# Gate and up of the shared MLP's first chunk as seven block products, in the last two token blocks

## Chip, cores and metric

The kernel runs on one core of a Trainium2 chip, in float32. The metric is the device time of one execution in microseconds (us). TensorE (PE) multiplies into PSUM, VectorE (DVE) and ScalarE (ACT) read PSUM and write SBUF, GpSimd (POOL) issues the indirect DMAs, and SyncE (SP) issues the others.

## What is computed

Two layers are applied to 2048 tokens of 512 features. The change touches the last part alone: the mixture-of-experts layer that ends the second one. Cut to what matters:

```
gu_s = x2 @ shared_w_gate_up.T            # shared MLP: 512 inner features
g_s, u_s = split(gu_s, 2)
shared_out = silu(g_s) * u_s @ shared_w_down.T
...                                       # router: top 2 of 16 experts
out_e = (silu(g) * u) @ w_down[e]         # 16 experts of 128 inner features
moe_out = einsum('eth,te->th', out_e, combine)
x = x + moe_out + shared_out
```

## The kernel before

**Tiles.** The tokens lie in four blocks of 512 columns (`tb` 0 to 3), the 512 features in four chunks of 128 partitions, all in one SBUF tile, `xall`. The shared MLP's 512 inner features are four chunks `j` of 128; `sw[j]` holds the weights of a chunk: columns 0 to 511 are gate, 512 to 1023 up, and the rest down.

**A chunk, plain.** `gate_up` (matmuls at L785) makes gate and up of chunk 0: two times four calls of 128x128 weights against 512 tokens, each result in one PSUM bank. A float32 call is two matmul instructions, so these are 16.

**A chunk from seven products.** Chunks 1 to 3 go through `seven`. Gate and up are taken as two rows of blocks, the features as two halves, the tokens as two halves of 256; the two-by-two block product is then seven block products and some additions (the scheme of Strassen in Winograd's form). It takes 14 calls against 256 tokens, 28 instructions (L1064). It needs sums of weight blocks, S2, S3 and S4, which `combine_shared(j)` makes with four DVE subtractions and additions, and differences of token blocks, `diffs[tb]`. The sum S1 is written over the first half of up in `sw[j]`, so that after `combine_shared(j)` a plain product of this chunk is no longer possible. The seven products come in four PSUM banks: the first is copied to SBUF by ACT (L1068), the others are added in by seven DVE instructions (L1070 to L1079).

**After either form,** ACT takes silu of gate (L1123), DVE multiplies by up (L1124), and `down` multiplies the result by the down weights, into four PSUM banks that gather all four chunks of a block (L1099; eight instructions a chunk). `down` of a chunk is issued after the products of the next, so that PE has work while ACT and DVE finish. At the end of a block DVE adds the four banks to the residual `x1` (L1144).

**Banks.** PSUM gives these stages three pools: `ps_mm` and `ps_td` of two banks each, taken in turn, and `ps_acc` of four for `down`. A plain chunk takes both banks of `ps_mm`; a chunk of seven products takes two of `ps_mm` and two of `ps_td`. A bank can be written again when its last reader is through.

**The end of the kernel, where the change lies.** Blocks 0 and 1 are computed earlier, beside the router. Then come the tiles of the experts (`worked`), which store their rows in `yd` in DRAM, and after them block 2, block 3 and the sum of the experts' rows. `shared(2, behind=sums)` and `shared(3, ...)` run the loop over `j` and call `sums(j)` after each chunk's product. For three rows of tokens or so at a time, `sums` weighs what was gathered (`weighed`: L1428, and L1429, which frees a buffer) and starts the next gathers (`rows_of`: a DVE memset of one column, L1419, then an indirect DMA on POOL, L1421; 32 gathers of 128 rows in all). The first six gathers are started ahead of block 2. The gathered tiles `g1` have six buffers, so a later gather waits for a weighing. `routed` runs midway through block 3: it transposes the weighed rows on PE (L1448, 64 instructions in 16 tiles, through `ps_mm` and `ps_td`) and DVE adds them to `x1` (L1449).

**Order.** Up to the experts, the order of PE, DVE and ACT is the program's own. From the experts on, a scheduler orders each engine's instructions; each engine then works its list from front to back. The weight sums of chunk 3, which were made early and put away in DRAM, are loaded again by SP (L1408) into a pool at the right end of SBUF, which lies where the experts' weights were.

Of the kernel before, what the change touches and what calls it, by code (L numbers as in the profile page):

```python
# [9 lines left out]
F32 = mybir.dt.float32  # L10
# [7 lines left out]
P = 128  # L18
# [11 lines left out]
NS1 = 4  # L30
# [13 lines left out]
BW = L // 2  # L44
# [59 lines left out]
def kernel(ctx: ExitStack, tc: tile.TileContext, a: dict, out: bass.AP):  # L104
    nc = tc.nc
    mm, tt, ts = nc.tensor.matmul, nc.vector.tensor_tensor, nc.vector.tensor_scalar
# [25 lines left out]
    s4 = wl0.tile([P, 5, H], F32, name="s4")  # L132
# [105 lines left out]
    def run(*streams):  # L238

        while streams:  # L240
            streams = [x for x in streams if next(x, run) is not run]
# [34 lines left out]
    start = small(1)  # L276
# [13 lines left out]
    pos = cst[:, C_POS : C_POS + NQ]  # L290
# [498 lines left out]
    def differ(g):  # L789
# [8 lines left out]
        tt(t3, b22, b12, ALU.subtract)  # L798
        tt(t4, b21, t2, ALU.subtract)

    def combine_shared(j):


        if j == NS1 - 1:
            assert len(ssw) == j - 1
            ssw.append(dif.tile([P, 4 * BW], F32, tag="t", name="ssw_made"))
        a11, a12, a21, a22 = (sw[j][:, i * BW : (i + 1) * BW] for i in range(4))
        s2, s3, s4 = (ssw[j - 1][:, i * BW : (i + 1) * BW] for i in range(3))
        yield tt(s3, a11, a21, ALU.subtract)
        yield tt(a21, a21, a22, ALU.add)  # L810
        yield tt(s2, a21, a11, ALU.subtract)
        yield tt(s4, a12, s2, ALU.subtract)
        if j == NS1 - 1:
            nc.sync.dma_start(shared_d, ssw[j - 1][:, 0 : 3 * BW])
# [59 lines left out]
    class Group:  # L874
# [6 lines left out]
        def down(self, j, at):  # L881
            for half in range(2):
                lo = half * TW
                for s in range(2):
                    mm(  # L885
                        self.zp[half][s][:, 0 : DW - TW],
                        at[:, 1 - half, :],
                        wn[:, j, s, lo : lo + DW - TW],
                        start=(j == 0),
                        stop=(j == NF - 1),  # L890
                    )
# [161 lines left out]
    def seven(tb, j, banks, si, at, done):  # L1053

        b11, b12, b21, b22 = quarters(tb)
        t1, t2, t3, t4 = diffs[tb]
        gate, up = (x.rearrange("p (k t) -> p k t", k=2) for x in (si, at))

        def products(k, *parts):
            ps = bank(banks[k % len(banks)], f"sgu_{tb}_{j}_{k}").rearrange("p (k t) -> p k t", k=2)  # L1060
            for i, (w, x) in enumerate(parts):
                w = sw[j][:, w * BW :] if w < 4 else ssw[j - 1][:, (w - 4) * BW :]
                for c in range(2):
                    mm(ps[:, i, :], w[:, c * P : (c + 1) * P], x[:, c, :], start=(c == 0), stop=(c == 1))  # L1064
            return ps

        ps = products(0, (0, b11), (6, b22))
        nc.scalar.copy(gate, ps)  # L1068
        ps = products(1, (1, b21), (4, t2))
        tt(up[:, 0], gate[:, 0], ps[:, 1], ALU.add)  # L1070
        tt(gate[:, 0], gate[:, 0], ps[:, 0], ALU.add)  # L1071
        tt(gate[:, 1], gate[:, 1], up[:, 0], ALU.add)
        done("gate", j)
        ps = products(2, (3, t4), (5, t3))
        tt(up[:, 1], up[:, 0], ps[:, 1], ALU.add)
        tt(up[:, 0], up[:, 1], ps[:, 0], ALU.add)  # L1076
        ps = products(3, (2, t1))
        tt(gate[:, 1], gate[:, 1], ps[:, 0], ALU.add)
        tt(up[:, 1], up[:, 1], ps[:, 0], ALU.add)  # L1079
# [3 lines left out]
    def shared(tb, behind=None, midway=None, hooks=None, first=None):  # L1083

        op = []
        hooks = hooks or {}

        def done(*step):  # L1090
            if step in hooks:
                hooks[step]()

        def down(j, at):
            if j == 0:
                op.extend(bank(ps_acc, f"op_{tb}_{o}") for o in range(NC))
            for o in range(NC):
                i = 2 * L + o * P
                mm(op[o], sw[j][:, i : i + P], at, start=(j == 0), stop=(j == NS1 - 1))  # L1099
            done("down", j)  # L1100

        before = None
        for j in range(NS1):
            if j > 0:
                si = glu.tile([P, TB], F32, tag="si", name=f"ssi_{tb}_{j}")
                at = glu.tile([P, TB], F32, tag="at", name=f"sat_{tb}_{j}")
                seven(tb, j, (ps_mm,) if hooks else (ps_mm, ps_mm, ps_td, ps_td), si, at, done)
                pair = [si, at]
            elif first is not None:
                pair = first()  # L1110
            else:
                banks = ps_mm if hooks else (ps_mm, ps_td)[j % 2]
                pair = []
                for which in range(2):
                    pair.append(bank(banks, f"sgu_{tb}_{j}_{which}"))
                    gate_up(pair[-1], tb, j, which)
                    if which == 0:
                        done("gate", j)
            done("products", j)
            if j == 0:  # L1120
                si = glu.tile([P, TB], F32, tag="si", name=f"ssi_{tb}_{j}")
                at = glu.tile([P, TB], F32, tag="at", name=f"sat_{tb}_{j}")
            nc.scalar.activation(si, pair[0], AF.Silu)  # L1123
            product = tt(at, si, pair[1], ALU.mult)  # L1124
            if j == 0 and tb == 1:
                diffs[tb] = in_place_of(0)
                run(differing(tb, diffs[tb]))
            if j == 0:
                x1 = pools[(1, 0, 2, 2)[tb]].tile([P, NC, TB], F32, tag="acc", name=f"x1_{tb}")
                nc.sync.dma_start(x1, x1d[tb])  # L1130
                acc.append(x1)
            done("up", j)
            if behind is not None:
                with tc.issue_after(product.ins):
                    behind(j)
            if before is not None:
                down(j - 1, before)
            before = at
            if j == 1 and midway is not None:
                midway()  # L1140
        down(NS1 - 1, before)

        for o in range(NC):
            tt(x1[:, o, :], x1[:, o, :], op[o], ALU.add)  # L1144
# [261 lines left out]
    late = ctx.enter_context(tc.tile_pool(name="late", bufs=1, side="right"))  # L1406
    ssw[-1] = late.tile([P, 3 * BW], F32, name="ssw_late")
    nc.sync.dma_start(ssw[-1], shared_d)  # L1408
    with tc.tile_pool(name="fin", bufs=NT) as fin:
        order = [q * NTB + tb for tb in range(NTB) for q in range(NTB)]  # L1410
        pairs = []

        def rows_of(lo, hi, held=True):

            for n in order[lo:hi]:
                g = [fin.tile([P, L], F32, tag=f"g{k}", name=f"g{k}_{n}", bufs=(NT, 6)[k]) for k in range(2)]
                for k in range(2):
                    if held:
                        nc.vector.memset(g[k][:, 0:1], 0.0)  # L1419
                    at = bass.IndirectOffsetOnAxis(ap=posi[:, k, n : n + 1], axis=0)  # L1420
                    nc.gpsimd.indirect_dma_start(g[k], None, yd[:, :], at)  # L1421
                pairs.append(g)

        def weighed(lo, hi):

            for i in range(lo, hi):
                n, g = order[i], pairs[i]
                ts(g[0], g[0], shr[:, 0, n : n + 1], None, ALU.mult)  # L1428
                stt(g[0], g[1], shr[:, 1, n : n + 1], g[0], ALU.mult, ALU.add)  # L1429

        cuts = (0, 0, 3, 6, 9, 13, NT)

        def sums(j):
            weighed(cuts[j], cuts[j + 1])
            rows_of(3 * (j + 1), min(3 * (j + 2), NT))

        rows_of(0, 3, held=False)
        shared(2, behind=sums)

        def routed():  # L1440

            for tb in range(NTB):
                for o in range(NC):
                    ps = bank((ps_mm, ps_td)[o % 2], f"moe_{tb}_{o}")
                    by_head = ps.rearrange("p (h b) -> p h b", b=B)
                    for q in range(4):
                        src = pairs[tb * 4 + q][0][:, o * P : (o + 1) * P]
                        nc.tensor.transpose(by_head[:, :, q * 2 * GB : (q + 1) * 2 * GB], src, ident)  # L1448
                    tt(acc[tb][:, o, :], acc[tb][:, o, :], ps, ALU.add)  # L1449
                    if tb < NTB - 1:  # L1450
                        nc.sync.dma_start(out[tb, :, o, :], acc[tb][:, o, :])

        shared(3, behind=lambda j: sums(4 + j) if j < 2 else None, midway=routed)
        for o in range(NC):
            nc.sync.dma_start(out[3, :, o, :], acc[3][:, o, :])
# [95 lines left out]
```

## Time and profile before

| | |
|---|---|
| median of 4 runs | 1032.94 us (1031.3 to 1036.56) |
| profiled execution, own time | 1031.51 us |
| its span | 1029.7 us |
| PE busy | 991.5 us, 96% |
| DVE busy | 648.2 us, 63% |
| ACT busy | 213.3 us, 21% |
| POOL busy | 169.8 us, 16% |
| mean granted PE clock | 0.998 |

The profile is of one execution. Its own time is 1.8 us more than its span, which goes from the first instruction to the last. Times in a row are in us from the span's start, unless marked ns. In a row of the timeline, the first number is the start and the second the time to the end of the last of its instructions; a bracket at the end tells how long the engine had been idle and what ended that. "remote" and "another core or an unknown queue" stand for a wait whose end the profile can't put down to an instruction that it has. Matmuls are pipelined, so their rows overlap: the step from one to the next is what one costs.

### The profile page before, as it was taken

The numbers are of one execution on the slowest core, as the hardware profiler recorded it, in microseconds if no ns is written. First come the engines' busy times: TensorE is split into PE (matmuls) and PEld (weight loads), VectorE is DVE, ScalarE is ACT, GpSimd is POOL, SyncE is SP. The second block draws the span as 40 slices with busy tenths as digits, with TensorE's granted clock in tenths as the row PEclk, the third lists the DMA queues.
The fourth block names the chain that finished last, engine by engine and source line by source line (L and its number), as shares of the span: only waits on it lengthen the run. The fifth ranks groups of instructions, "written<-read, shape, count | busy, mean of one in ns | idle before, by whom it ended". The sixth has DMA issues, their size and how long they took to land. (4 is left out here: it accounts for less than half of the span.)

```text
span 1029.7 us, 16926 instructions
## 1 busy us (share of the span) xinstructions
PE 991.5 (96%) x6256; PEld 792.8 (77%) x6256; DVE 648.2 (63%) x1974; ACT 213.3 (21%) x439; POOL 169.8 (16%) x189
## 2 busy tenths in 40 slices
PE   3999999999999999999999999999999999999898
PEld 1777656888898889988899888897757777776566
DVE  6655567886666776666766757775864443334485
ACT  2322111121221311223112122212101222221000
POOL 2131001210301202102012021000001222223530
PEclk9999999999999999999999999999999999999999
DMA  6666408685656756746467466532920455546452
GB/s 183 194 218 230 134 21 303 232 295 176 224 183 195 243 165 210 252 154 232 150 219 256 161 200 229 180 108 71 417 120 23 133 167 170 172 156 217 140 175 98
DMA packets 64210, 190.62 MB, mean 185 GB/s; under 512 B 8512, under 2 KB 11616, under 8 KB 63488
## 3 DMA queue, kind: packets, MB, share of 16 engines
q1 hardware_dynamic: 49360, 138.30, 39.1%
q0 software_dynamic: 14176, 51.16, 15.9%
q8 instruction: 52, 0.85, 0.3%
q14 instruction: 30, 0.25, 0.1%
q10 hardware_dynamic: 592, 0.07, 0.1%
HBM read 158.35 MB, written 31.15 MB: 184 GB/s over the span
## 5 line engine op out<-in xcount | busy, mean ns | idle before, releaser
L885 PE MATMUL zp<-wn,at 128*128 128x288 f32 x704 | 185.4, 406 | 0.4 <-DVE at L984 0.4
L819 PE MATMUL gu<-t,w 128*128 128x128 f32 x1056 | 150.6, 279 | 1.0 <-DVE gus L966 0.9
L885 PEld LDWEIGHTS zp<-wn,at 128*128 128x128 f32 x704 | 127.1, 190 | 28.6 <-DVE at L984 0.6
L819 PEld LDWEIGHTS gu<-t,w 128*128 128x128 f32 x1056 | 134.8, 191 | 16.4 <-DVE gus L966 8.6
L444 POOL DMA_INDIRECT wa<-in_la,row_a x64 | 61.4, 959 | 305.3 <-issue 185.1
L982 ACT ACTIVATE si<-gus 128x256 f32<-128x256 f32 x88 | 36.8, 418 | 346.6 <-DVE gus L980 346.6
L819 PE MATMUL gum<-xall,w 128*128 128x128 f32 x704 | 93.3, 275 | 0.0
L819 PEld LDWEIGHTS gum<-xall,w 128*128 128x128 f32 x704 | 85.6, 192 | 0.0
L960 DVE TENSOR_TENSOR los<-los 128x512 f32<-128x512 f32 (+1 forms) x72 | 46.6, 647 | 55.9 <-ACT los L839 54.1
L1327 PE MATMUL egu<-wall,zx 128*128 x336 | 80.6, 383 | 0.4 <-issue 0.4
L1327 PEld LDWEIGHTS egu<-wall,zx 128*128 128x128 f32 x336 | 60.5, 189 | 20.0 <-ACT zx L1318 10.4
L966 DVE TENSOR_TENSOR gus<-gu,los 128x512 f32<-128x512 f32 x88 | 60.6, 689 | 23.8 <-PE gu L819 11.0
L984 DVE TENSOR_TENSOR at<-si,gus 128x256 f32<-128x256 f32 x88 | 37.5, 426 | 48.4 <-ACT si L982 47.3
L1308 POOL DMA_INDIRECT zr<-zd,tok x42 | 39.8, 948 | 159.4 <-PE zrp L1316 86.3
L839 ACT COPY los<-lo 128x512 f32<-128x512 f32 (+1 forms) x96 | 47.5, 558 | 65.3 <-PE lo L836 62.2
L1099 PE MATMUL op<-sat,sw 128*128 128x512 f32 x128 | 58.3, 596 | 2.7 <-DVE sat L1124 2.4
L589 PE MATMUL main<-yT,w 128*128 128x512 f32 x128 | 58.4, 599 | 0.0
L836 PEld LDWEIGHTS lo<-rs,wb 64*128 64x128 f32 x704 | 42.6, 187 | 17.0 <-issue 11.2
L836 PE MATMUL lo<-rs,wb 64*128 64x128 f32 x704 | 48.0, 279 | 6.9 <-DVE gus L980 6.2
L819 PE MATMUL gu<-xall,w 128*128 128x128 f32 x352 | 53.7, 275 | 0.0
L819 PE MATMUL gum<-t,w 128*128 128x128 f32 x352 | 53.7, 275 | 0.0
L1347 DVE COPY eys<-ey 128x512 f32<-128x512 f32 x42 | 29.1, 692 | 29.7 <-PE ey L1345 29.7
(316 smaller groups left out, 1456.3 us busy)
## 6 DMA issues: line engine op xcount, KB each, us to landing
w<-sums_d SPq DMA_DIRECT2D x77, 512.0 KB
w<-in_cw SPq DMA_DIRECT2D x77, 384.0 KB
wall<-in_xw SPq DMA_DIRECT2D x16, 768.0 KB
yd<-eys SPq DMA_DIRECT2D x42, 256.0 KB
g<-kpad SPq DMA_DIRECT2D x15, 512.0 KB
w<-in_cw SPq DMA_DIRECT2D x11, 512.0 KB
sums_d<-w SPq DMA_DIRECT2D x9, 512.0 KB
xall<-in_xT SPq DMA_DIRECT2D x4, 1024.0 KB
```

The costliest lines, as they stand in the source:

```text
L444: nc.gpsimd.indirect_dma_start(to, None, src, at)
L589: mm(ps, w0[:, c, o * P : (o + 1) * P], yT[:, c, :], start=(c == 0), stop=(c == NC - 1),)
L819: mm(to, block(n, i)[:, c * P : (c + 1) * P], x[:, c], start=(c == 0), stop=(c == 1))
L836: mm(banks[which][:, at : at + P], wb[mine, lo : lo + P], r[mine, half, :], start=True, stop=True)
L839: nc.scalar.copy(to[:, first - j : first - j + n, 2 * which : 2 * which + 2], src)
L885: mm(self.zp[half][s][:, 0 : DW - TW], at[:, 1 - half, :], wn[:, j, s, lo : lo + DW - TW], start=(j == 0), stop=(j == NF - 1),)
L960: tt(lo[:, :, i], lo[:, :, i], lo[:, :, less], ALU.subtract)
L966: tt(flat, ps, adapters[:, j % 4].rearrange("p k t -> p (k t)"), ALU.add)
L984: tt(at, si, flat[:, TG:], ALU.mult)
L1099: mm(op[o], sw[j][:, i : i + P], at, start=(j == 0), stop=(j == NS1 - 1))
L1308: nc.gpsimd.indirect_dma_start(zr, None, zd[:, :], bass.IndirectOffsetOnAxis(ap=tok[:, t : t + 1], axis=0))
L1327: mm(ps[:, 0:256], x[:, c, :], wflat()[:, bass.ds(start + c * 256, 256)], start=(c == 0), stop=(c == NC - 1))
```

## The change

Block 2 now takes its chunks in the order 1, 2, 0, 3. After the product of its first chunk (chunk 1), DVE makes the weight sums of chunk 0, from the weights in SBUF, into a new tile, `ssw_first`. Chunk 0 of block 2 (now third) and of block 3 (still first) then go through `seven` as the other chunks do. Blocks 0 and 1 keep the plain form. `sums`, the load of `x1` and `routed` go by a chunk's position in the order, no longer by its number.

```diff
+    first_sums = []
+
+    def sums_of(j):
+        return ssw[j - 1] if j > 0 else first_sums[0]
+
     def combine_shared(j):
...
-        s2, s3, s4 = (ssw[j - 1][:, i * BW : (i + 1) * BW] for i in range(3))
+        s2, s3, s4 = (sums_of(j)[:, i * BW : (i + 1) * BW] for i in range(3))
         yield tt(s3, a11, a21, ALU.subtract)
         yield tt(a21, a21, a22, ALU.add)
         yield tt(s2, a21, a11, ALU.subtract)
...
-                w = sw[j][:, w * BW :] if w < 4 else ssw[j - 1][:, (w - 4) * BW :]
+                w = sw[j][:, w * BW :] if w < 4 else sums_of(j)[:, (w - 4) * BW :]
...
+        order = (1, 2, 0, 3) if tb == 2 else range(NS1)
+
         def down(j, at):
-            if j == 0:
+            if not op:
                 op.extend(bank(ps_acc, f"op_{tb}_{o}") for o in range(NC))
             for o in range(NC):
                 i = 2 * L + o * P
-                mm(op[o], sw[j][:, i : i + P], at, start=(j == 0), stop=(j == NS1 - 1))
+                mm(op[o], sw[j][:, i : i + P], at, start=(j == order[0]), stop=(j == order[-1]))
             done("down", j)
...
-        for j in range(NS1):
-            if j > 0:
+        for pos, j in enumerate(order):
+            plain = j == 0 and tb < 2
+            if not plain:
...
                 seven(tb, j, (ps_mm,) if hooks else (ps_mm, ps_mm, ps_td, ps_td), si, at, done)
...
-            if j == 0:
+            if plain:
                 si = glu.tile([P, TB], F32, tag="si", name=f"ssi_{tb}_{j}")
...
-            if j == 0:
+            if pos == 0:
                 x1 = pools[(1, 0, 2, 2)[tb]].tile([P, NC, TB], F32, tag="acc", name=f"x1_{tb}")
                 nc.sync.dma_start(x1, x1d[tb])
...
                 with tc.issue_after(product.ins):
-                    behind(j)
+                    behind(pos)
             if before is not None:
-                down(j - 1, before)
+                down(order[pos - 1], before)
             before = at
-            if j == 1 and midway is not None:
+            if pos == 1 and midway is not None:
                 midway()
-        down(NS1 - 1, before)
+        down(order[-1], before)
...
     nc.sync.dma_start(ssw[-1], shared_d)
+    first_sums.append(late.tile([P, 3 * BW], F32, name="ssw_first"))
...
-        shared(2, behind=sums)
+        def first_then_sums(j):
+            if j == 0:
+                run(combine_shared(0))
+            sums(j)
+
+        shared(2, behind=first_then_sums)
```

## The prediction

> **What bounds the kernel now.** The page comes first: PE is busy 96% of the span, so the time is the length of PE's work plus the places where PE stands still. The change lies behind the experts, so the second view is the busy time by stretch: block 2 (932.70 to 979.54 us), block 3 up to the end of `routed` (to 1006.37), and the rest, with a piece of the second stretch by itself. The columns are the stretch, its length, then busy time and count of PE, PEld, DVE, ACT and POOL, the granted clock, the DMA share and GB/s.
>
> ```profile
> 932.70:979.54 46.84, 41.78 (x137) 26.50 (x135) 22.70 (x71) 4.14 (x7) 23.94 (x24) 0.96 0.59 190
> 979.54:1006.37 26.83, 26.83 (x125) 18.01 (x123) 21.84 (x43) 1.81 (x3) 7.59 (x8) 1.00 0.59 192
> 1006.37:1029.70 23.33, 19.23 (x75) 13.60 (x73) 11.01 (x23) 2.44 (x4) 0.00 (x0) 0.99 0.19 69
> ...
> 997.40:1006.40 9.00, 9.00 (x60) 6.69 (x59) 9.00 (x16) 0.00 (x0) 0.00 (x0) 1.00 0.78 290
> ```
>
> Two things are to be seen. In block 2 PE is idle for 5.06 of 46.84 us and its clock is below 1. In the last 9 us of `routed` DVE is as full as PE.
>
> The chain of waits tells why block 2 ends when it does (start, length, what).
>
> ```profile
> 951.98 11.23 another core or an unknown queue
> 963.30 0.42 DVE sat L1070
> ...
> 964.52 1.56 another core or an unknown queue
> 966.10 0.43 DVE sat L1075
> ...
> 975.25 0.70 DVE sat L1124
> 976.00 3.70 PE op L1099 x8
> 979.70 6.87 PE sgu L785 x16
> 986.57 6.04 PE sgu L1064 x28
> ```
>
> DVE stands still for 11.23 us ahead of the first addition of the block's third chunk, and 1.56 us later. The products it needs were issued on PE at 951.63 and 953.36, so PE was long through. I call this the **hold**: what PE finished at about 953 and 955 us is seen by DVE at 963.2 and 966.1. Its cause isn't in the profile. What stands beside it is a stream of 18 gathers on POOL, back to back from 940.62 to 963.36; their queue is 64% busy from 962 to 964 us and 18% from 964 to 970. A second stream, 12 gathers from 971.57 to 987.00, has no hold.
>
> PE's timeline shows what the hold costs.
>
> ```profile
> 960.25 1.03 PE L1064 MATMUL sgu<-xall,ssw_late 128*128 128x256 f32 x4
> 964.23 2.07 PE L1064 MATMUL sgu<-xall,sw 128*128 128x256 f32 x4 [2.96 <-issue]
> 966.10 1.78 PE L1064 MATMUL sgu<-xall,ssw_late 128*128 128x256 f32 x4
> 967.71 1.03 PE L1064 MATMUL sgu<-xall,sw 128*128 128x256 f32 x4
> ...
> 976.00 3.70 PE L1099 MATMUL op<-sat,sw 128*128 128x512 f32 x8 [2.10 <-DVE sat L1124]
> ```
>
> PE waits 2.96 us for a bank that DVE hasn't read; the next eight matmuls take 967.71 - 964.23 = 3.48 us instead of 8 x 0.216 = 1.73; and PE waits 2.10 us for the last `down`. Together 2.96 + 1.75 + 2.10 = 6.81 us.
>
> **The change, part by part.** *Products.* Each of the two blocks loses 16 instructions of L785 (6.87 us in the chain, 0.429 each) and gains 28 of L1064 (6.04 us, 0.216 each). That is 0.83 us less PE work in each block, 1.66 in both. PSUM banks: two products move to `ps_td`, whose last readers ahead of both places are done.
>
> *DVE and ACT.* Each block gains seven DVE additions of 128x256 (0.42 us in their row, 2.9 in all) and one copy on ACT (0.59). What matters is when the chunk's product is ready, since `weighed` is queued behind it on DVE. For a chunk alone, the timeline of DVE and PE has it:
>
> ```profile
> 986.67 0.69 DVE L1124 TENSOR_TENSOR sat<-ssi,sgu 128x512 f32<-128x512 f32 x1 [4.82 <-issue]
> ...
> 1006.48 1.03 PE L1064 MATMUL sgu<-xall,sw 128*128 128x256 f32 x4
> ...
> 1013.90 0.69 DVE L1124 TENSOR_TENSOR sat<-ssi,sat 128x512 f32<-128x512 f32 x1 [0.43 <-ACT ssi L1123]
> ```
>
> From PE's start of a chunk of seven to its product are 1013.90 - 1006.48 = 7.42 us. In block 3, where PE starts at 979.54, the product then starts at 986.96, not 986.67: 0.29 us late. The other additions fall into the 4.82 us in which DVE is idle today.
>
> *Sums of chunk 0.* Four DVE instructions of 128x256, 4 x 0.42 = 1.7 us once, in the list between the products of chunks 1 and 2. PE starts chunk 1 in effect at 933.6 (932.70, and 0.86 for the last experts' matmul that stands among its first ones), so its product ends at about 933.6 + 7.42 + 0.69 = 941.7, and the sums by 943.5. Chunk 2's additions can start when its second product is through, at 933.6 + 6.04 + 3.46 + 0.1 = 943.2, and are 0.3 us late, which the products behind cover. PE needs the sums at 933.6 + 2 x 6.04 + 3.43 (a `down`) + 0.86 = 950.0, within the first product of chunk 0: 6.5 us of cover, so nothing. Six memsets for gathers 7 to 12 stand between them, at 942 to 943.5 instead of 941.34; POOL comes to the first of these gathers at 948.14, so 4.6 us of cover. The third row of `weighed` still waits for its gather, as now (950.58). SP's and POOL's lists keep their order, and no DMA is added.
>
> [...] The gathers beside SBUF-only work of DVE take longer in the trace:
>
> ```profile
> 946.89 0.95 POOL L1421 DMA_INDIRECT g<-yd,posi  x1 [0.30 <-issue]
> 948.14 1.32 POOL L1421 DMA_INDIRECT g<-yd,posi  x1 [0.30 <-issue]
> 949.76 1.06 POOL L1421 DMA_INDIRECT g<-yd,posi  x1 [0.30 <-issue]
> ```
>
> Beside five such instructions of `weighed` two gathers together lose 0.48 us. [...] By the row it is 4/5 of 0.48, 0.4 us, for the first stream; nothing on the path waits for these gathers, so I add nothing.
>
> *Block 2 in sum.* PE comes 0.83 us sooner to the point where it waits for a bank. DVE frees the bank only after the hold. Bounds: 0, if the hold ends at a fixed time with the gathers, and 0.83, if it moves with PE; below nothing, 1.7 by the second rival. I take 0, since the gathers don't move. Behind the hold the same list follows (additions, three weighings, additions, product), so the last `down` starts at 976.0 as now.
>
> *Block 3 in sum.* From 986.67 to 1007.7 DVE has hardly a gap, so it ends `routed` 0.29 us later. PE would come to the products of chunk 2 at 1006.48 - 0.83 = 1005.65, but needs a bank of `ps_mm`, freed by the 13th of the 16 additions of L1449. The first starts at 997.41, the other 15 run from 998.67 in steps of 0.60, so this one ends at 998.67 + 11 x 0.60 + 0.69 = 1005.96 today, at 1006.25 after. PE starts at about 1006.3: 0.18 us sooner, and 0.65 of the 0.83 is lost to DVE.
>
> **Sum:** 0 + 0.18 = 0.2 us less: 1031.3 for an execution like the profiled one. That one is 1.4 us under the median of the four runs, so I forecast **1032.7 us** as the median.
>
> **Rivals.** *The hold is gone.* It shows once in two streams of gathers, and the change gives the third chunk other instructions at other times. Against it: all runs before lie between 1031.3 and 1036.56, none near 1024, so it seems to come each time; and the first stream stays as it is. It would give back 6.81, and 0.83 + 0.18 of the change's own: 7.8 us less, 1025.1. It is faster by 0.76%.
>
> *A second spell of half clock.* The matmuls after PE's idle time of 2.96 us took 0.427 us instead of 0.216; after 2.10 us ahead of the last `down` they didn't. If PE works off its 0.83 us ahead of that wait while DVE doesn't move, the idle time is 2.93, next to the bad one. The spell lasted 3.4 us and costs half of it, 1.7: 1.5 us slower in all, 1034.4. It decides between 2.10 and 2.96 us. [...]
>
> *A hold in the second stream.* These 12 gathers run beside chunk 0 of block 3, which now has three more results for DVE to wait for. The first hold ended 2.7 us behind the last issue of its stream (963.36 to 966.1). One from 983.2, where the first addition is due, to 987.0 + 2.7 = 989.7 costs up to 6.5 us, and the weighings and `routed` stand behind it on DVE: 1032.7 + 6.5 = 1039.2. It decides as soon as DVE's first addition starts later than 984. Today ACT's silu starts there in time, which speaks against it.
>
> *The change doesn't do what it says.* The lists of instructions exclude this: PE, DVE and ACT differ only from block 2 on, DVE by 7 + 7 + 4 instructions.
>
> **Numbers.** Hold as now, 0.55: 1032.7, and 1031 to 1035 with the scatter of the runs. Hold gone or most of it, 0.26: 1025.1. Half clock, 0.10: 1034.4. Hold in the second stream, 0.09: 1039.2. Leaving out the last and the tails, the range is 1024.2 to 1036.5. Half a per cent, 5.2 us, is about what a measurement of this kernel can tell from no change. Faster by more: the second case nearly whole, 0.25. Slower by more: the last and some scatter, 0.09. Within: 0.66.
>
> **What would show it.** Right: L785 is gone behind 932 us, a chunk 0 takes 6.04 us on PE, DVE's unknown wait stands ahead of chunk 0 in block 2 and ends near 963, PE's idle time there grows to about 3.8 us, and DVE's additions in `routed` end near 1008. Wrong: block 2 ends at other than 979.5, by the hold (earlier) or by matmuls at 0.43 us per 256 tokens behind the last wait (later).

## The result and the profile after

The changed kernel took **1035.71 us** (median of 44 runs, 1029.30 to 1042.82); the kernel before, beside it, 1033.63 us (median of 70 runs). The ratio is **1.0014, 95% interval 1.0004 to 1.0023**: slower by 0.14%, about 1.4 us. Forecast were 0.2 us less. The profiled execution took 1032.96 us, with a span of 1031.2 us.

The same three stretches as in the prediction: block 2, block 3 up to the products of its third chunk, and the rest (stretch, length, busy time of PE, PEld, DVE, ACT and POOL, clock, DMA share, GB/s).

```profile
932.17:979.58 47.41, 41.55 (x147) 27.98 (x147) 28.66 (x84) 4.76 (x8) 25.18 (x25) 0.96 0.61 194
979.58:1007.83 28.25, 27.14 (x137) 20.17 (x136) 22.83 (x48) 2.32 (x4) 6.63 (x7) 1.00 0.51 166
1007.83:1031.20 23.37, 19.22 (x73) 13.60 (x72) 11.40 (x23) 2.43 (x4) 0.00 (x0) 1.00 0.21 75
```

From PE's first product on, block 2 is 0.57 us longer, though PE is busy 0.23 us less in it. (Counted from the last expert's matmul, which ended 0.96 us earlier here, it is 45.25 us against 44.26.) Block 3, which I had 0.18 us shorter, takes 28.25 us to the products of its third chunk, where the kernel before took 1006.48 - 979.54 = 26.94. That is the loss: 1.31 us.

In block 2 the hold is there again, but it comes in portions. The seven products of a chunk come in four banks; by its first to fourth result I mean these banks, and by a signal what tells DVE or ACT that PE is through with one. DVE's timeline, the first addition on each of the three results that it waits for (start, length, what, idle time before and what ended it):

```profile
954.33 0.42 DVE L1075 TENSOR_TENSOR sat<-ssi,sgu 128x256 f32<-128x256 f32 x1 [3.32 <-PE sgu L1069]
...
961.29 0.42 DVE L1080 TENSOR_TENSOR sat<-sat,sgu 128x256 f32<-128x256 f32 x1 [5.75 <-PE sgu L1069]
...
965.52 0.42 DVE L1083 TENSOR_TENSOR ssi<-ssi,sgu 128x256 f32<-128x256 f32 x1 [3.36 <-remote]
```

PE had started on these banks at 950.27, 952.00 and 953.73 and was through with all at 954.75. The 18 gathers ran from 940.00 to 963.0. So the hold ends 2.5 us behind the end of the last of them, much as before (2.7). On PE's timeline the last `down` of the block then falls into half clock (granted clock 0.50 from 974.60 to 977.00 us):

```profile
967.45 3.70 PE L1107 MATMUL op<-sat,sw 128*128 128x512 f32 x8
974.64 5.11 PE L1107 MATMUL op<-sat,sw 128*128 128x512 f32 x8 [3.49 <-DVE sat L1133]
979.58 1.03 PE L1069 MATMUL sgu<-xall,sw 128*128 128x256 f32 x4
```

Eight matmuls take 5.11 us instead of 3.70 after 3.49 us of idle time: 1.41 us more, where the second rival had 1.7. With it block 2 ends at 979.58, where it did before.

In block 3 the chain of waits (start, length, what) goes through the first chunk's additions, and later from DVE's additions of `routed` back to PE:

```profile
979.75 6.14 PE sgu L1069 x28
985.90 0.43 DVE sat L1080
986.36 0.42 DVE sat L1081
986.78 0.54 another core or an unknown queue
987.34 0.43 DVE ssi L1083
...
998.86 0.48 DVE g L1438
999.34 0.61 DVE x L1464
999.99 0.66 PE moe L1463 x4
```

PE started the chunk at 979.58, so the third result was through at 979.58 + 24 x 0.216 = 984.76 and the fourth at 985.62. DVE takes them at 985.90 and 987.34, 1.1 and 1.7 us later. The second stream of gathers runs beside them, from 970.20 to 985.62. DVE's product of silu and up for this chunk starts at 988.52, which is 8.94 us behind PE's start, not 7.42. From there to the additions of `routed` DVE has hardly a gap.

### The profile page after: what moved, and what is told of

It is laid out like the page before. It is cut to its first block, busy times and chain, and to the rows that moved or that the text cites. A ratio compares the mean times of both kernels' runs of the same rounds, so it can differ in the third digit from the quotient of the medians.

```text
span 1031.2 us, 16997 instructions
## 1 busy us (share of the span) xinstructions
PE 991.2 (96%) x6280; PEld 796.5 (77%) x6280; DVE 655.2 (64%) x1992; ACT 214.3 (21%) x441; POOL 170.0 (16%) x189
## 5 line engine op out<-in xcount | busy, mean ns | idle before, releaser
L1069 PE MATMUL sgu<-xall,sw 128*128 128x256 f32 x200 | 51.5, 382 | 0.8 <-issue 0.6
```

## The experiments

I call the chips A (of the comparison above) and B to F, one for each set of runs. Every set ran beside the kernel before on the same chip. A ratio is the time over that of this kernel before, and behind it stands its 95% interval.

**First set, chip B: which half loses.** The two kernels again, and the change in one block alone. Edits of the latter two to the changed kernel:

```diff
 block 3 alone
-        order = (1, 2, 0, 3) if tb == 2 else range(NS1)
+        order = range(NS1)
-            plain = j == 0 and tb < 2
+            plain = j == 0 and tb < 3
-            if j == 0:
+            if j == 1:
                 run(combine_shared(0))
 block 2 alone
-            plain = j == 0 and tb < 2
+            plain = j == 0 and tb != 2
...
+            if j == 3:
+                a21, a22 = (sw[0][:, i * BW : (i + 1) * BW] for i in (2, 3))
+                tt(a21, a21, a22, ALU.subtract)
```

> The kernel before against itself, for the scatter and for the granted clock of each execution. Profiled executions so far: after is 1.5 us longer, 0.6 of it in block 2 (a spell of half clock at the last down) and 1.3 behind the start of block 3 (additions of routed 1.8 us late on DVE), less 0.5 that the start of block 2 happened to be early. Theory A, half clock and late DVE: ratio 1.000; the executions differ by the number of half-clock spells, so their time falls by about 1.1 us for each 0.001 of mean clock, as it does in the 46 executions of the changed kernel (slope -1126 us per 1.0), and the median clock is higher than that of the changed kernel. Theory B, late DVE alone: same slope, but the median clock is that of the changed kernel.

> The changed kernel again, beside the kernel before on one chip. Theory A: ratio 1.0010 to 1.0020, median clock lower than before's by 0.001 to 0.0017 (one spell of 3.4 us at half clock in 1031 us is 0.00165). Theory B: the same ratio at the same clock. Rival C, the gain and loss are both scatter: ratio within 0.0005 of 1.

> Chunk 0 from seven products in block 3 alone; block 2 plain and in the order 0 to 3, the four sums made behind its second chunk. My forecast's term was 0.18 us less. Theory A and B: block 3 loses what it lost in the changed kernel, 1.3 us from its start to the products of chunk 2 (28.25 us instead of 26.94), because the chunk's product is late on DVE: ratio 1.0010 to 1.0015. Rival D, the late last product of that chunk (its end seen 1.5 us late) was an accident of the one execution: product 0.3 us late, ratio 0.9995 to 1.0000.

> Chunk 0 from seven products in block 2 alone (one more DVE subtraction at the end of block 2 gives the chunk's plain weights back), block 3 plain. My forecast's term was 0. Theory A: the last down of block 2 falls into half clock (5.1 us for eight matmuls instead of 3.6) and block 2 is 0 to 0.6 us longer: ratio 1.0000 to 1.0006. Theory B: block 2 is neither longer nor shorter by over 0.3 us and the last down runs at 3.6 us. Rival E, block 2 gains its 0.83 us in most executions and only the profiled one missed it: ratio 0.9992.

Measured, ratios to the kernel before (median of 35 runs 1032.08 us): itself 0.9991 (0.9975 to 1.0007), changed 1.0003 (0.9981 to 1.0026), block 3 alone 1.0043 (1.0024 to 1.0061), block 2 alone 0.9996 (0.9975 to 1.0017). The changed kernel's 1.0003 can't be told from no change, so on this chip the loss itself isn't shown in the times: Theories A and B had 1.0010 to 1.0020, Rival C a value within 0.0005 of 1. The mean clock of the changed kernel's 12 executions was 0.9968, of the 35 before 0.9965. So half-clock spells aren't more frequent with the change here, and **Theory A's forecast of a lower clock fails**. For chip A the clocks of the kernel before aren't on record, but for one execution, so a share of such spells in the 1.4 us there can't be excluded. The profile of the changed kernel has the late results again, later than on A; PE started block 3 at 976.94:

```profile
984.72 0.42 DVE L1080 TENSOR_TENSOR sat<-sat,sgu 128x256 f32<-128x256 f32 x1 [2.30 <-remote]
...
987.32 0.69 DVE L1133 TENSOR_TENSOR sat<-ssi,sat 128x512 f32<-128x512 f32 x1 [0.43 <-ACT ssi L1132]
```

Its block 3 took 29.69 us, 2.76 more than before, but its block 2 was 2.75 us shorter: that the ratio there lies near the forecast is luck. With block 2 alone changed, block 2 was 0.53 us shorter in the profile and its last `down` ran at 3.70 us; the interval is too wide to tell Theory B from Rival E.

Block 3 alone didn't isolate what it should. Its hold lasted longest of these four, until 976.5, and the rows tell why. One row each of POOL's, DVE's and PE's timeline of that kernel:

```profile
972.66 0.95 POOL L1431 DMA_INDIRECT g<-yd,posi  x1 [0.30 <-issue]
```

```profile
976.54 0.42 DVE L1075 TENSOR_TENSOR sat<-ssi,sgu 128x256 f32<-128x256 f32 x1 [11.79 <-remote]
```

```profile
980.37 5.53 PE L1107 MATMUL op<-sat,sw 128*128 128x512 f32 x8 [8.59 <-DVE sat L1133]
```

Here the third chunk's additions came through early, DVE weighed rows early, and POOL went on without a pause: 24 gathers to 973.61 instead of 18. The hold ended 2.9 us behind them. So it goes with the stream of gathers, and its price is set by what DVE lets POOL start. That kernel's second stream was 6 gathers long and over at 990.71, before the third result of block 3 was due (990.92). Its product came 7.42 us behind PE's start, 0.29 us late as Rival D had it, and its block 3 took 26.74 us, as forecast. This speaks against the change's DVE work as such being the loss.

**Second set, chip C: shorter streams, and none.** In both kernels; "paced" starts the gathers behind later weighings, "plain loads" replaces them:

```diff
 paced
-            rows_of(3 * (j + 1), min(3 * (j + 2), NT))
+            if j > 0:
+                rows_of(4 * j - 1, min(4 * j + 3, NT))
 plain loads
-                    nc.gpsimd.indirect_dma_start(g[k], None, yd[:, :], at)
+                    t = NTU - 1 - (n if k else 0)
+                    nc.sync.dma_start(g[k], yd[t * P : (t + 1) * P, :])
```

> The kernel before with the same gathers in shorter streams: three rows, then four behind the weighing of each of three chunks, then one (6, 8, 8, 8, 2 gathers instead of 18, 12, 2). Theory S, signals of finished products are held while a long stream of POOL gathers runs, until 1.1 to 3.0 us behind its last gather: with no stream over 8 (about 10 us) no DVE wait of over 2 us for a product that PE ended, PE idle in block 2 down from 5.1 us to under 2, no spell of half clock: 5 to 7 us less, ratio 0.993 to 0.996. Rival P, the hold comes from something else in block 2 (PE's, DVE's or the DMAs' load): DVE waits as before, ratio 0.999 to 1.001. Rival Q, the gathers come too late for their weighings, and DVE waits for DMA instead: ratio 0.998 to 1.004.

> The changed kernel with the same shorter streams. Theory S: without the hold the change is worth 0.83 us in block 2, and in block 3 what its 0.3 us of late product leaves (0.18): 0.5 to 1.2 us below the paced kernel before. Theory T, the loss in block 3 is DVE's own (seven additions and a copy more), with or without the streams: block 3 takes 28.0 to 29.5 us from its start to the products of chunk 2, as in the changed kernel, and the kernel is not below the paced kernel before.

> The kernel before with plain loads of 128 whole rows on SP's queue in place of all 32 gathers of POOL; the rows that are weighed and added are then not those that the routing chose, the bytes and everything else are as before. Theory S (the hold needs POOL's gathers): no DVE wait of over 2 us for a product that PE ended, PE idle in block 2 under 2 us; ratio 0.993 to 0.996. Rival P (the load of the DMAs holds the signals, whoever issues them): waits as before, ratio 0.999 to 1.001.

> The changed kernel with plain loads on SP's queue in place of the gathers (the rows weighed and added are not those that the routing chose). Theory S: 0.5 to 1.2 us below the kernel before with plain loads, 0.83 of it in block 2; block 3 takes 26.6 to 27.0 us from its start to the products of chunk 2. Theory T: block 3 takes 28.0 to 29.5 us, no gain on the kernel before with plain loads. Rival P: as the changed kernel, ratio 1.000 to 1.002.

Measured beside 1035.42 us: paced before 1.0020 (1.0000 to 1.0039), paced changed 0.9996 (0.9979 to 1.0012), plain loads before **0.9932** (0.9910 to 0.9955), plain loads changed **0.9894** (0.9870 to 0.9919). The pacing failed: without the early hold the weighings came sooner, and the pieces ran together into streams of 16 and 24. DVE's rows of the paced kernel before, whose 16 gathers ended at 976.15:

```profile
975.59 0.42 DVE L1075 TENSOR_TENSOR sat<-sat,sgu 128x256 f32<-128x256 f32 x1 [4.43 <-remote]
...
978.45 0.42 DVE L1078 TENSOR_TENSOR ssi<-ssi,sgu 128x256 f32<-128x256 f32 x1 [1.98 <-remote]
```

Again the hold ends behind its stream, 2.3 us. In the paced changed kernel it moved into block 3, where PE stood still for 8.76 us. Block 2 of that kernel took 36.61 us, as without a hold, though a stream of 24 gathers ran beside it from 952.95 on: signals aren't held all the time that a stream runs. With plain loads the hold is gone. PE's timeline of the kernel before with plain loads has the last two `down` in one row, without a gap:

```profile
966.39 7.03 PE L1099 MATMUL op<-sat,sw 128*128 128x512 f32 x16
973.26 7.03 PE L785 MATMUL sgu<-xall,sw 128*128 128x512 f32 x16
```

The bytes alone don't hold the signals (Rival P), since the same bytes move; Rival Q shows in DVE waits of under 1.5 us for gathers only. Theory T falls: with plain loads the changed kernel's block 3 takes 26.74 us. Without the hold, its sections are shorter than those of the kernel before with plain loads, block 2 by 0.40 us and block 3 by 0.19 (the rest 0.20 longer). The times, 1024.67 us in 5 runs against 1027.69 in 6, point the same way, but their intervals overlap.

**Third set, chip D.** Plain loads issued by POOL; the first multiplication of each weighing on ACT; five POOL memsets behind each eight gathers (in the changed kernel and the one before).

```diff
 plain loads by POOL
-                    nc.gpsimd.indirect_dma_start(g[k], None, yd[:, :], at)
+                    nc.gpsimd.dma_start(g[k], yd[t * P : (t + 1) * P, :])
 on ACT
-                ts(g[0], g[0], shr[:, 0, n : n + 1], None, ALU.mult)
+                nc.scalar.activation(g[0], g[0], AF.Copy, scale=shr[:, 0, n : n + 1])
 pauses
+                    if gathers and len(gathers) % 8 == 0:
+                        with tc.issue_after(gathers[-1].ins):
+                            for _ in range(5):
+                                behind = nc.gpsimd.memset(rest, 0.0)
```

> The kernel before with plain loads of 128 whole rows in place of the 32 gathers, now issued by POOL on its own queue (the rows weighed and added are not those that the routing chose). On SP's queue they left no hold, and block 2 took 37.0 us behind the last expert instead of 44.3 to 45.2. Theory S1, what holds the signals is POOL's own writing of transfers: waits of DVE of 4 to 14 us as before, block 2 44 to 46 us, ratio 0.998 to 1.002. Theory S2, it takes the gather with its list of rows: no such wait, block 2 37 us, ratio 0.992 to 0.995.

> The changed kernel with the first multiplication of each weighed row on ACT instead of DVE (16 of 0.40 us off DVE, 7 of them in block 3). Theory U, in block 3 the changed kernel is late because DVE gets its last product 1.5 to 2.6 us late and then has no gap until the additions of routed: with 2.8 us less work there block 3 takes 26.7 to 27.2 us to the products of chunk 2 instead of 28.3 to 29.7, and block 2 is 1.2 us shorter behind the hold; 2 to 4 us less than the changed kernel, ratio 0.9965 to 0.9995. Rival V, DVE's load is not it (the late product itself keeps PE waiting): block 3 stays at 28 to 29.7 us, ratio 1.000 to 1.002.

> The kernel before with five POOL memsets (estimated at 2 to 3 us together, from 0.24 us for one of 127 columns) behind each eight gathers, so that no stream is longer than eight. The kernels paced by DVE's memsets ran their pieces together into streams of 16 and 24, and the hold moved with the end of the stream (978.45 behind 976.15; 987.99 behind 984.27). Theory S: pieces of eight, 10 us, end before the first signal is late (11 us and more behind the start of a stream so far); no DVE wait of over 2 us on a finished product, block 2 37 to 39 us; ratio 0.993 to 0.996. Rival W, a pause of this length does not clear what holds the signals: the hold lasts to the end of the second or third piece, block 2 as before or longer, ratio 0.999 to 1.005.

> The changed kernel with the same pauses of POOL. Theory S: without the hold the change gives its 0.83 us in block 2 and 0.2 in block 3: 0.5 to 1.2 us below the kernel before with pauses; ratio 0.992 to 0.995. Rival W: held in the second or third piece; ratio 0.999 to 1.006, with the loss in block 2 or 3 where the signals are due.

Measured: the kernel before took **1019.66 us** here, 12 us less than on chip B. Ratios: plain loads by POOL 1.0002 (0.9992 to 1.0012), ACT 1.0148 (1.0127 to 1.0170), pauses before 1.0039 (1.0025 to 1.0054), pauses changed 1.0024 (1.0007 to 1.0042). None of the four profiles has a hold, and taking the gathers away gained nothing, so on this chip there is none to remove. The pauses, 2.9 to 3.0 us of memsets each in the kernel before, only make the last rows late: in the changed kernel DVE waits 6.2 us for them, and block 3 took 30.8 us (30.9 in the kernel before). Theory S and Rival W can't be told apart here, nor S1 and S2. ACT lost by its own order: it came to the weighings ahead of the silu and waited for gathers with the silu behind them:

```profile
961.32 0.72 ACT L1438 ACTIVATE g<-g,shr 128x512 f32<-128x512 f32 x1 [1.84 <-DMA g<-yd,posi]
961.95 0.61 ACT L1132 ACTIVATE ssi<-ssi 128x512 f32<-128x512 f32 x1
```

**Fourth set, chip E: both kernels where there is no hold.** The ACT version now has `tc.issue_after(silu.ins)` around its weighings.

> The kernel before against itself, with its profile on this chip: whether this chip shows the hold. On three chips the kernel before took 1031.5 to 1035.4 us, and its profiles there show DVE waiting 4 to 14 us for finished products in block 2 (44.3 and 45.2 us long). On a fourth it took 1019.7 us, and three kernels profiled there show no such wait. Theory X, the hold belongs to some chips or their state: a time near 1020 comes with a block 2 of 37 us, a time of 1031 and more with one of 44 to 46 us. Rival: no such pairing.

> The changed kernel on the same chip. Theory X: with the hold, ratio 1.000 to 1.003 and block 3 of 28.2 to 29.7 us; on a chip without it the change gives what it takes off PE: block 2 36.6 us, block 3 26.7, ratio 0.9985 to 0.9995 (0.5 to 1.5 us less). Rival Y, the loss in block 3 (last product of its first chunk seen late on DVE) comes without the hold in block 2 too: ratio 1.000 to 1.002 on either sort of chip.

> The changed kernel with the first multiplication of each weighed row on ACT, now put behind the chunk's silu (in the try before, ACT stood before the silu and waited 1 to 6 us for gathers, and block 2 took 51.2 us). Theory U, block 3 is late because DVE has no gap up to the additions of routed: block 3 with the tail behind it is 49.5 to 50.2 us, instead of 51.6 to 53.1 in the changed kernel with the hold (50.2 in the kernel before); 1.5 to 3 us less than the changed kernel on this chip if it has the hold, 0 to 0.6 us less if not. Rival V, DVE's load is not it: block 3 with the tail stays as in the changed kernel.

> The changed kernel with plain loads issued by POOL in place of the gathers (the rows weighed and added are not those that the routing chose). If this chip has the hold, Theory S1 (POOL's own writing of transfers holds the signals) gives DVE waits of 4 to 10 us and the time of the changed kernel within 2 us; Theory S2 (it takes the gathers) gives a block 2 of 36.6 us without such waits and 5 to 9 us less than the changed kernel. Without the hold on this chip both give the time of the changed kernel within 1 us.

Measured beside 1020.14 us: the kernel before 0.9995 (0.9981 to 1.0009), **changed 0.9988 (0.9979 to 0.9998)**, with ACT 0.9973 (0.9963 to 0.9983), plain loads by POOL 0.9987 (0.9977 to 0.9997). Chip E has no hold, and there the change is faster, though the interval ends only just below 1. What is missing isn't the stream: the kernel before issued 30 gathers without a pause from 936.2 to 974.7, longer than any stream above, and DVE took every product at once. Two rows of DVE for the fourth chunk of its block 2, which PE started at 954.95:

```profile
958.67 0.42 DVE L1070 TENSOR_TENSOR sat<-ssi,sgu 128x256 f32<-128x256 f32 x1 [1.52 <-PE sgu L1064]
...
960.33 0.42 DVE L1075 TENSOR_TENSOR sat<-sat,sgu 128x256 f32<-128x256 f32 x1 [0.41 <-PE sgu L1064]
```

And the first chunk of block 3 in the changed kernel, which PE started at 966.88, so that the third result was through at 972.06; the product is 7.42 us behind PE's start:

```profile
972.26 0.42 DVE L1080 TENSOR_TENSOR sat<-sat,sgu 128x256 f32<-128x256 f32 x1 [0.44 <-PE sgu L1069]
...
974.30 0.69 DVE L1133 TENSOR_TENSOR sat<-ssi,sat 128x512 f32<-128x512 f32 x1 [0.42 <-ACT ssi L1132]
```

**Fifth set, chip F.** The ACT version of both kernels.

> The changed kernel with the first multiplications on ACT behind the chunk's silu, once more, on whatever chip comes. On one without the hold, as measured: ratio 0.996 to 0.998. On one with the hold, Theory U (the late last product of block 3's first chunk costs time because DVE has no gap behind it): block 3 with its tail 49.5 to 50.2 us, ratio 0.996 to 0.999, below the changed kernel's 1.0014. Rival V: block 3 with its tail 51.5 us and more, ratio 1.000 to 1.002.

> The kernel before with the same multiplications on ACT. Without the hold: block 2 stays at 37.0 us and block 3 with its tail loses 0.2 to 0.6 us less than in the changed kernel, since there DVE has less to do in it: ratio 0.998 to 0.999, so the changed kernel's version is below it by 0.5 to 1.2 us. With the hold: block 2 is 1.2 us shorter (three multiplications less between the hold's end and the last product), ratio 0.998 to 0.9995, and if Theory U holds the changed kernel's version is not above it.

Measured beside 1034.14 us: changed with ACT 1.0020 (1.0001 to 1.0040), before with ACT 1.0002 (0.9982 to 1.0023). The hold is there: in block 2 of the first DVE waits 6.89 and 6.46 us for finished products. Block 3 with what follows it took 52.31 us in the first and 50.23 in the second. Theory U's number fails, and Rival V's holds (51.5 us and more, 1.000 to 1.002): with 2.8 us less on DVE the late product still costs its lateness. The forecast for the second kernel, 0.998 to 0.9995, missed too. DVE's rows of the first (its third result was through at 977.59 + 5.18 = 982.77):

```profile
986.05 0.42 DVE L1080 TENSOR_TENSOR sat<-sat,sgu 128x256 f32<-128x256 f32 x1 [2.97 <-PE sgu L1069]
...
988.02 0.69 DVE L1133 TENSOR_TENSOR sat<-ssi,sat 128x512 f32<-128x512 f32 x1 [0.43 <-ACT ssi L1132]
```

**All sets in one table.** Block 2 is counted from the end of the last expert's matmul on PE, block 3 to the products of its third chunk; "product" is the time from PE's start of block 3 to DVE's product of its first chunk.

| kernel, chip | block 2 | product | block 3 | rest |
|---|---|---|---|---|
| before, A | 44.26 | 7.13 | 26.94 | 23.22 |
| before, B | 45.15 | 7.14 | 26.93 | 23.24 |
| block 2 alone, B | 44.62 | 7.14 | 26.94 | 23.28 |
| **changed, A** | 45.25 | **8.94** | **28.25** | 23.37 |
| **changed, B** | 42.40 | **10.38** | **29.69** | 23.37 |
| block 3 alone, B | 48.69 | 7.42 | 26.74 | 23.32 |
| paced before, C | 46.72 | 7.14 | 26.94 | 23.23 |
| paced changed, C | 36.61 | 18.03 | 38.14 | 23.32 |
| plain loads before, C | 37.01 | 7.14 | 26.93 | 23.71 |
| plain loads changed, C | 36.61 | 7.43 | 26.74 | 23.91 |
| before, E | 37.01 | 7.14 | 26.93 | 23.31 |
| changed, E | 36.61 | 7.42 | 26.73 | 23.39 |
| changed with ACT, E | 36.61 | 7.42 | 24.43 | 24.97 |
| changed with ACT, F | 43.44 | 10.43 | 27.31 | 25.00 |
| before with ACT, F | 43.07 | 7.14 | 25.23 | 25.00 |

The column "product" settles where block 3 loses. Without lateness the changed kernel takes 26.73 us; with 8.94 - 7.42 = 1.52 us of lateness it takes 28.25 (1.52 more), with 10.38 - 7.42 = 2.96 it takes 29.69 (2.96 more). All of the lateness arrives at the end of the block.

The new results don't come later in the stream than the plain chunk's, so that isn't the reason. On chip B the stream of 12 started 7.97 us ahead of block 3 in both kernels (971.36 and 968.97). The plain chunk's second result was through 14.8 us behind the stream's start and DVE took it at once; the third result of the seven products was through 13.2 us behind the start, and DVE took it 2.6 us later.

## Why the prediction was wrong

**Products: right.** Chip E shows all of it. Block 2 is 0.40 us shorter behind the last expert, and 0.42 less of its products stands ahead of that point (1.30 us, six matmuls of 0.216, instead of 1.72, four of 0.429): together 0.82, forecast 0.83. Block 3 is 0.20 shorter, forecast 0.18, by the very route given (product at 7.42 us instead of 7.14). The rest grows by 0.08. In sum 0.94 us less by sections, and 0.0012 x 1020 = 1.2 us (0.2 to 2.1) by the ratio.

**Sums: right.** Nothing waits for them, and two gathers beside them took 1.05 and 1.07 us on chip A instead of 0.95, in all 0.22 us more (0.38 on chip E). My row said 0.4.

**Block 2 in sum: the mean is not settled.** I took the hold as ending at a fixed time behind the gathers. That it goes with them is shown (on chips A, B and C it ends 1.1 to 3.1 us behind the last, at 964 to 987 us). But its length differs by more than the change is worth: 45.25 and 42.40 us for the same changed kernel on A and B. The half-clock rival was what happened in the first profile, at the price of 1.41 us; in the second, the last `down` ran at 3.70 us behind 1.36 us of idle time, and the one ahead of it took 4.98. My rule that an idle time between 2.10 and 2.96 us decides doesn't carry over either: on chip B the kernel before had its spell (four matmuls in 2.07 us instead of 1.03) behind idle times of 1.02, 1.50 and 1.64 us. So the length of one gap alone doesn't tell: a gap of 2.10 us on chip A passed without a spell.

**Block 3 in sum: this step failed.** "The product then starts at 986.96, not 986.67: 0.29 us late" took PE's signals there as seen at once. In all three profiles of the seven products beside the stream of 12 gathers on a chip with the hold they weren't (8.94, 10.38 and 10.43 us instead of 7.42); on E, beside a stream as well, they were. So the 0.18 us of gain in the sum was a loss of 1.31 us in the profiled execution. That is the third rival, to which I gave 0.09. My argument against it, that ACT's silu starts there in time, held for the plain chunk alone: in all four profiles of it beside that stream on a chip with the hold its product is on time, 7.13 to 7.14 us. Its deciding point was wrong too: DVE's first addition started at 983.30, 981.21 and 981.87, ahead of 984, and it was the third result that came late. The lateness was 1.5 to 3.0 us, not up to 6.5. Block 3 as a whole lost 1.3 and 2.8 us on A and B. With nothing from block 2, as I forecast, the lower of these is about the 1.4 us (0.4 to 2.4) by which the change is slower on A; what block 2 adds or gives back isn't settled.

**Shown and not shown.** Shown: in every profile with the hold and the stream of 12, the seven products of block 3 are seen 1.5 to 3.0 us late and the block is longer by that; without the hold, on chip E, the change gains, and with plain loads on C its sections do. The loss in time is shown on chip A alone. Only argued: that block 2's mean is unchanged with the hold, and with it how much of the 1.4 us is block 3's. Open: what holds the signals; why the seven products fall into it in block 3 and the plain chunk doesn't (the plain one gives DVE and ACT two results to wait for, not four, but that wasn't tried alone); whether it takes gathers or any transfer issued by POOL (the two runs for it came on chips without the hold).

**A better version** is the changed kernel with ACT on a chip without the hold, 0.9973 against 0.9988 without ACT; on chip F it isn't better than the kernel before (1.0020). What ACT gives the kernel before on a chip without the hold wasn't measured.

## What to carry to other kernels

A form with fewer multiplications and more intermediate results can cost more in signals than it saves (block 3 here: 0.20 us saved on E, 1.3 and 2.8 us lost on A and B): count how many finished results the next engine must see, and look whether a transfer stream runs beside them that already makes signals late. Where an engine's list is without a gap from a product to the end of a block, each us by which that product is late was here a us of the block, and less work later in the list (ACT on F) didn't give it back. Measure on more than one chip before a sign is believed that is smaller than what chips differ by.

## What the runs showed of the hardware

Times differ by chip, or by what else differed from set to set: each set was one chip at one time. On A, B, C and F the kernel before took 1032.1 to 1035.4 us and on D and E 1019.7 and 1020.1. Of this, 7.2 to 8.1 us is block 2 (44.26 and 45.15 against 37.01), and the last expert ends 3.3 to 4.4 us later (934.18 and 935.28 against 930.85), for a reason that wasn't looked into. In the profiles of both kernels on A and of the kernel before on B the rows on transfers have no time from issue to landing, in that of the kernel before on E they have it (3.8 us for these gathers); whether the recording itself takes part in the hold wasn't tried.

Time goes with the clock: over 46 executions of the changed kernel on chip A (mean granted clock 0.990 to 1.000) a straight line through them falls by 1.1 us for each 0.001.
